# Another written order for the attention and feed-forward stage of a four-stage kernel

## The chip, the cores and the metric

The kernel runs on one core of one Trainium2 chip. A core has five engines that play their own instruction streams side by side: TensorE (PE in the profile; its weight loads are listed apart as PEld), VectorE (DVE), ScalarE (ACT), GpSimd (POOL), and SyncE (SP), which here only issues DMAs. The metric is the device time of one execution in microseconds (us), the median over the runs of one kernel.

## The reference

A sequence of 2048 tokens with 128 channels passes four blocks, each added to its own input. The first is an oscillating recurrence, the second a gated choice among 8 experts, the third a causal attention over 256 tokens. The fourth, which takes two thirds of the time and which the change touches, has six layers of local attention and a feed-forward network:

```python
def attn_layer(x, Wqkv, qs, ksc, Wo):                 # 16 heads of 64
    q, k, v = jnp.split(x @ Wqkv, 3, -1)              # then split into heads
    q, k = l2norm(q) * qs, l2norm(k) * ksc
    q = q * cos * scale + rotate_half(q) * sin * scale
    k = k * cos * inv + rotate_half(k) * sin * inv
    out = local_attention(q, k, v)                    # windows of 32, each sees itself and the one before
    return out @ Wo
...
def ffn_layer(x, g, bln, W1, b1, W2, b2):
    hg = layernorm(x, g, bln) @ W1 + b1
    a, gate = jnp.split(hg, 2, -1)
    return a * jax.nn.gelu(gate, approximate=False) @ W2 + b2
...
for i in range(DEPTH):                                # 6
    x = attn_layer(shift_tokens(x), ...) + x
    x = ffn_layer(shift_tokens(x), ...) + x
```

`shift_tokens` delays half of the channels by one token. All arithmetic of this block is float32.

## The kernel before

Stages 1 to 3 run first and are the same in both kernels. `stage4` keeps the activations transposed (channels on the partitions) in two buffers `s4[0]` (input of a layer) and `s4[1]` (between attention and feed-forward). The tokens are cut into 16 tiles of 128 (`NT`), so that six layers make 96 tiles, and four tiles make a group (`G`), the unit of the feed-forward part.

For each tile there are small step functions (lines 1044 to 1274). Each emits a handful of instructions on one engine:

- `ps` (PE, four matmuls): q and k from `wqkv`; the first digit in a step's name is 0 for q and 1 for k, the second the half. `sq`, `ss` (ScalarE, VectorE): squares and their sums per head; `rn` (POOL): the norms' inverse, a power; `ra`, `rb` (VectorE) and `rs` (POOL): the rotation; `kn` (POOL): k times its norm. `tab` (POOL) makes the rotation's table.
- `pt` (PE, 8 transposes each for q and k), `qT`, `kT` (ScalarE): their copies out of PSUM; `ca` (POOL): the window carried to the next tile.
- `pv` (PE): v; `vt` (ScalarE): its copy; `vw` (SP): v through DRAM into the layout of the windows, by six DMAs.
- `sc` (PE, 128 small matmuls): the scores; `sm`, `mx` (VectorE): mask and maximum; `nb` (POOL); `ex` (ScalarE): 16 exponentials, one for each head; `su`, `nr` (VectorE): sum and division.
- `ptp` (PE, 8 transposes), `pT` (ScalarE): the weights transposed; `po` (PE, 128 small matmuls in four steps `po0` to `po3`): the weighing of v; `oT` (ScalarE): its copy.
- `px` (PE, 64 matmuls for two tiles, so in every other iteration; four steps): the output projection; `s` (VectorE): the residual sum.

For each group (lines 1276 to 1380): `xt` (PE), `xs` (VectorE), `fr` (POOL), `prb` (PE), `xcn` (VectorE): layer norm; `ph` (PE, two matmuls for each of three chunks 0 to 2), `ge` (ScalarE), `act` (the function `gated`, VectorE): the gated hidden layer; `py` (PE, one step for each chunk): the second product; `s2` (VectorE): the sum; `st` (`store`, last layer only: four transposes on PE called `pst`, a copy and a DMA). `bias` runs once a layer.

What sets the order of the work is the list `steps` in `stage4`: pairs of a step and its lag. The loop at its end plays the whole list for each iteration i from 0 to 111; a step with lag d works on tile t = i - d, and a step of a group only where t is a multiple of four. So each iteration is a slice through a pipeline that is 16 tiles deep. Which group steps an iteration holds depends on i mod 4, and `px` plays where t is odd. The helper `InOrder` (line 66) keeps each engine's instructions exactly in the written order, so there is no scheduler that moves them, and the profile shows line 66 for all of them; the tile names tell them apart.

The engines' streams are joined by semaphores and by buffers that come round. All results of PE in stage 4 go through one pool of four PSUM buffers of two banks each, which the tag "big" (line 1037) hands out in the order of the calls: `ps`, `pv`, `pt`, `sc`, `ptp`, `po`, `px`, `xt`, `prb`, `ph`, `py`, `pst` share it. A buffer comes free when its last reader (a copy, mask or sum) is done. Work tiles of ScalarE and VectorE come from a pool of eight (line 1040).

Of the kernel before, what the change touches and what calls it, by code (L numbers as in the profile page):

```python
# [93 lines left out]
class Kernel:  # L94
# [893 lines left out]
    def stage4(self, x3T, out):  # L988
        nc, tc, a = self.nc, self.tc, self.a
        with ExitStack() as ctx:  # L990
# [42 lines left out]
            st = [{} for _ in range(DEPTH * NT + 1)]  # L1033
# [348 lines left out]
            def of(f, *n):  # L1382
                return lambda t: f(t, *n)

            tiles = dict(
                tab=tab, rn=rn, kn=kn, vt=vt, vw=vw, pt0=of(pt, 0), qT=qT, pt1=of(pt, 1), kT=kT, ca=ca,
                sm=sm, mx=mx, nb=nb, ex=ex, su=su, nr=nr, ptp=ptp, pT=pT, oT=oT, s=s,
# [10 lines left out]
            for n in range(3):  # L1398
# [5 lines left out]


            steps = [
                ("ps00", 0), ("pT", 4), ("ps01", 0), ("ph21", 14), ("mx", 3), ("py0", 15), ("xcn", 11), ("rn", 2),
                ("py1", 15), ("nb", 3), ("py2", 15), ("sq0", 0), ("ra1", 1), ("po0", 4), ("po1", 4), ("ge2", 14),
                ("ex", 3), ("rb1", 1), ("rb0", 0), ("po2", 4), ("kn", 2), ("s2", 15), ("tab", -1), ("px0", 5),
                ("px1", 5), ("st", 15), ("px2", 5), ("ra0", 0), ("ph00", 13), ("xt", 9), ("act2", 14), ("xs", 9),  # L1410
                ("ss1", 1), ("px3", 5), ("po3", 4), ("s", 5), ("pt1", 2), ("kT", 2), ("vw", 3), ("ph10", 11),
                ("ph01", 13), ("pt0", 1), ("ph11", 11), ("ca", 3), ("ss0", 1), ("oT", 4), ("pv0", 2), ("qT", 1),
                ("pv1", 2), ("su", 3), ("sc0", 2), ("rs1", 1), ("sc1", 2), ("nr", 3), ("vt", 2), ("sc2", 2),
                ("sc3", 2), ("ge1", 11), ("ge0", 13), ("sm", 2), ("ps10", 0), ("act0", 13), ("ps11", 0),
                ("prb", 10), ("fr", 9), ("act1", 11), ("ph20", 13), ("ptp", 3), ("sq1", 0), ("rs0", 0),
            ]
            last = DEPTH * NT
            self.wo4 = {}
# [121 lines left out]
```

## Time and profile before

| | |
|---|---|
| median of three runs | 2450.68 us (2450.47 to 2456.15) |
| the profiled execution's own time | 2441.8 us |
| its span, from first to last instruction | 2439.8 us |
| TensorE's mean granted clock | 0.969 |
| busy: PE, DVE, ACT, POOL | 91%, 78%, 70%, 64% |
| matmuls on PE | 39448 |
| of stage 4: `ps`, `po`, `pt`, `px` | 768, 12288, 1536, 3072 matmuls |
| DMA | 193.83 MB, mean 79 GB/s |

The profile is of one execution, taken by the hardware profiler. It gives each engine's busy time, the waits with what ended them (the releaser), and a chain of work that ended last, followed back from the last instruction. "issue" means an engine waited for nothing that the profile shows. Three kinds of answers of the trace are used below: sums over a stretch of time, lists of the waits in it, and a timeline, in which neighbouring instructions of one kind are folded into a row with start, duration, engine, operation, result and operands, their partitions and shapes, how many there were, and in brackets the idle time before the first.

### The profile page before, as it was taken

Reading aid. Unit: us, or ns where it says so; the run is one execution under the profiler, and the core shown is the slowest. Engines: PE = TensorE matmul, PEld = TensorE weight load, DVE = VectorE, ACT = ScalarE, POOL = GpSimd, SP = SyncE. Lnnn points to the kernel's source line nnn. Section 1 sums busy time; section 2 is a strip of 40 time slices with the busy share of each in tenths; the row PEclk is TensorE's granted clock in tenths of the full one; section 3 lists DMA queues with packets and bytes.
Section 4 is the critical chain, followed back from the end, with each engine's and each line's share of the span. In section 5 each row is a group of like instructions: output and inputs, shape, how many; then the busy total and the mean of one; then the engine's idle time right before and its main releaser. Section 6 shows DMA issues by size and latency. Waiting matters only on the chain.

```text
span 2439.8 us, 88508 instructions
## 1 busy us (share of the span) xinstructions
PE 2229.9 (91%) x39448; PEld 1380.0 (57%) x39448; DVE 1902.5 (78%) x2743; ACT 1707.6 (70%) x3209; POOL 1573.5 (64%) x1205
## 2 busy tenths in 40 slices
PE   5678889999997799999999999999999999999997
PEld 3663333333334466666666666666666666666664
DVE  7667777776652788888888888888888787888875
ACT  3323455666664678888788888888888787888873
POOL 4244210001122999888888888888888788888870
PEclk8788999999998899999999999999999999999999
DMA  2000000000001544354344444453435443343331
GB/s 82 1 1 1 1 1 2 2 2 2 2 2 44 131 115 115 106 144 111 106 106 141 114 110 120 123 132 104 113 106 136 104 120 98 104 115 107 105 101 50
DMA packets 101021, 193.83 MB, mean 79 GB/s; under 512 B 11480, under 2 KB 32608, under 8 KB 100640
## 3 DMA queue, kind: packets, MB, share of 16 engines
q1 hardware_dynamic: 100060, 187.71, 28.1%
q8 instruction: 310, 5.08, 0.9%
q14 instruction: 71, 0.58, 0.1%
q10 hardware_dynamic: 580, 0.46, 0.1%
HBM read 124.17 MB, written 63.96 MB: 77 GB/s over the span
## 4 chain that ended last, share of the span: by engine, by line
PE 57%; ACT 2%; issue 1%; DVE 1%; POOL 1%; ACTq 0%
PE ps L66 13%; PE po L66 8%; PE px L66 7%; PE pv L66 6%; PE pt L66 6%; PE sc L66 5%; PE ph L66 5%; PE ptp L66 3%; PE py L66 3%; ACT sm L66 1%; PE prb L66 1%; ACT kT L66 1%; PE xt L66 0%; DVE s L66 0%; DVE yT L66 0%
## 5 line engine op out<-in xcount | busy, mean ns | idle before, releaser
L66 POOL TENSOR_TENSOR rn<-ss,mhalf 128x32 f32<-128x32 f32 x96 | 523.9, 5457 | 8.0
L66 ACT ACTIVATE sm<-sm,mx,rn 128x64 f32<-128x64 f32 x1536 | 519.1, 428 | 2.3 <-POOL mx L66 1.8
L66 POOL TENSOR_TENSOR rot_a<-rot_a,rot_b 128x1024 f32<-128x1024 f32 x192 | 452.8, 2371 | 14.5 <-DVE rot_a L66 13.4
L66 DVE TENSOR_REDUCE mx<-sc 128x1 f32<-128x512 f32 (+3 forms) x640 | 355.1, 604 | 120.9 <-PE sc L66 114.0
L66 ACT ACTIVATE ex<-sc 128x512 f32<-128x512 f32 (+3 forms) x640 | 302.9, 536 | 198.8 <-PE sc L66 197.5
L66 PE MATMUL sc<-kT,qT 64*32 64x64 f32 (+3 forms) x14208 | 375.0, 243 | 28.8 <-issue 21.3
L66 PE MATMUL ps<-wqkv,s 128*128 128x512 f32 x768 | 376.4, 613 | 6.3 <-DVE vec L66 2.4
L66 ACT ACTIVATE sq<-ps 128x1024 f32<-128x1024 f32 x192 | 196.6, 1024 | 218.5 <-issue 113.0
L66 PE MATMUL sc<-qT,kT 32*128 32x512 bf16 (+3 forms) x1920 | 248.4, 348 | 23.7 <-DVE mx L66 16.2
L66 DVE TENSOR_TENSOR rot_b<-ps,tab 128x1024 f32<-128x1024 f32 x192 | 229.8, 1216 | 24.6 <-ACT sq L66 22.9
L66 DVE TENSOR_TENSOR rot_a<-ps,tab 128x1024 f32<-128x1024 f32 x192 | 233.5, 1217 | 17.1 <-ACT sq L66 16.5
L66 PEld LDWEIGHTS po<-pT,vw 64*64 64x64 f32 x12288 | 195.6, 135 | 86.6 <-ACT pT L66 41.1
L66 DVE TENSOR_REDUCE ss<-sq 128x16 f32<-128x1024 f32 x192 | 228.4, 1211 | 1.4
L66 PE MATMUL po<-pT,vw 64*64 64x32 f32 x12288 | 214.6, 220 | 3.7 <-ACT pT L66 2.6
L66 PE MATMUL pt<-ident,rot_a 128*128 128x128 f32 x1536 | 199.6, 279 | 15.3 <-POOL rot_a L66 15.3
L66 POOL TENSOR_SCALAR_AFFINE_SELECT ex<-ex 128x512 f32<-128x512 f32 x64 | 40.6, 635 | 267.6 <-ACT ex L66 267.4
L66 PE MATMUL pv<-wqkv,s 128*128 128x512 f32 x384 | 184.0, 602 | 21.1 <-ACT kT L66 20.8
L66 PEld LDWEIGHTS pt<-ident,rot_a 128*128 128x128 f32 x1536 | 172.4, 142 | 45.4 <-issue 18.5
L66 PEld LDWEIGHTS ps<-wqkv,s 128*128 128x128 f32 x768 | 132.2, 192 | 112.9 <-issue 100.1
L66 PE MATMUL px<-oT,wo 64*128 64x128 f32 x3072 | 187.7, 277 | 1.9 <-issue 1.9
L66 PEld LDWEIGHTS sc<-kT,qT 64*32 64x32 f32 x12288 | 128.4, 105 | 101.1 <-issue 89.3
L66 PE MATMUL av<-ex,va 128*32 128x256 f32 (+1 forms) x2432 | 178.5, 372 | 5.0 <-POOL ex L66 5.0
(225 smaller groups left out, 3679.1 us busy)
## 6 DMA issues: line engine op xcount, KB each, us to landing
vw<-vd SPq DMA_DIRECT2D x384, 256.0 KB
vd<-vt SPq DMA_DIRECT2D x96, 512.0 KB
vd<-vt SPq DMA_DIRECT2D x90, 128.0 KB
wqkv<-in_L_ffn_Wqkv SPq DMA_DIRECT2D x18, 512.0 KB
wo<-in_L_ffn_Wo SPq DMA_DIRECT2D x24, 256.0 KB
w<-in_L_ffn_W SPq DMA_DIRECT2D x6, 341.0 KB
x<-in_L_attn_hidden_states SPq DMA_DIRECT2D x4, 256.0 KB
out<-ot SPq DMA_DIRECT2D x4, 256.0 KB
```

What stands on the lines that cost most here:

```text
L66: return self._tc.keep_in_program_order(call(*args, **kw))
```

## The change

Only the list `steps` changes: the order of its entries and some of the lags. Every step is still played once for each tile or group, so both kernels issue the same instructions on the same data, except where a step of one iteration is now played in a neighbouring one.

- `px` stands ahead of `po`, and `po0` to `po3` follow one another; before, `px` stood between `po2` and `po3`. Where i mod 4 is 1, `ph21` stands in the middle of `po`.
- `ph20` stands at the start of an iteration instead of the end, `ph21` has lag 13 instead of 14, `ph00` and `ph01` stand behind `sc` instead of around `xt` and `pt`. `py0` has lag 14 instead of 15. `prb` stands at the start.
- `mx` and `nb` have lag 2 instead of 3, `rn` 1 instead of 2, `pT` 3 instead of 4, each at the end of the iteration instead of near its start; `ss0` has lag 0 instead of 1, `rs0` 1 instead of 0, `xcn` 10 instead of 11, `ge2` and `act2` 13 instead of 14.
- Other entries (`s`, `s2`, `st`, `xs`, `fr`, `ca`, `tab`, `kn`, `qT`, `su`) stand elsewhere in the list with the same lag; the store stands behind `vw` instead of ahead of it.

```diff
--- before.py
+++ after.py
@@ -1404,15 +1404,15 @@
 
 
             steps = [
-                ("ps00", 0), ("pT", 4), ("ps01", 0), ("ph21", 14), ("mx", 3), ("py0", 15), ("xcn", 11), ("rn", 2),
-                ("py1", 15), ("nb", 3), ("py2", 15), ("sq0", 0), ("ra1", 1), ("po0", 4), ("po1", 4), ("ge2", 14),
-                ("ex", 3), ("rb1", 1), ("rb0", 0), ("po2", 4), ("kn", 2), ("s2", 15), ("tab", -1), ("px0", 5),
-                ("px1", 5), ("st", 15), ("px2", 5), ("ra0", 0), ("ph00", 13), ("xt", 9), ("act2", 14), ("xs", 9),
-                ("ss1", 1), ("px3", 5), ("po3", 4), ("s", 5), ("pt1", 2), ("kT", 2), ("vw", 3), ("ph10", 11),
-                ("ph01", 13), ("pt0", 1), ("ph11", 11), ("ca", 3), ("ss0", 1), ("oT", 4), ("pv0", 2), ("qT", 1),
-                ("pv1", 2), ("su", 3), ("sc0", 2), ("rs1", 1), ("sc1", 2), ("nr", 3), ("vt", 2), ("sc2", 2),
-                ("sc3", 2), ("ge1", 11), ("ge0", 13), ("sm", 2), ("ps10", 0), ("act0", 13), ("ps11", 0),
-                ("prb", 10), ("fr", 9), ("act1", 11), ("ph20", 13), ("ptp", 3), ("sq1", 0), ("rs0", 0),
+                ("ps00", 0), ("ps01", 0), ("prb", 10), ("ra1", 1), ("kn", 2), ("ph20", 13), ("rb1", 1), ("rs0", 1),
+                ("tab", -1), ("sq0", 0), ("ca", 3), ("px0", 5), ("py1", 15), ("ex", 3), ("px1", 5), ("py2", 15),
+                ("ra0", 0), ("rs1", 1), ("rb0", 0), ("xt", 9), ("px2", 5), ("px3", 5), ("po0", 4), ("po1", 4),
+                ("ph21", 13), ("po2", 4), ("po3", 4), ("pt1", 2), ("xs", 9), ("xcn", 10), ("fr", 9), ("vw", 3),
+                ("s", 5), ("s2", 15), ("st", 15), ("py0", 14), ("ph10", 11), ("kT", 2), ("ss1", 1), ("pt0", 1),
+                ("oT", 4), ("ph11", 11), ("pv0", 2), ("pv1", 2), ("ss0", 0), ("sc0", 2), ("sc1", 2), ("sc2", 2),
+                ("su", 3), ("qT", 1), ("sc3", 2), ("nr", 3), ("vt", 2), ("ge2", 13), ("sm", 2), ("ph00", 13),
+                ("ge1", 11), ("mx", 2), ("rn", 1), ("ph01", 13), ("ps10", 0), ("ge0", 13), ("ps11", 0),
+                ("act2", 13), ("act0", 13), ("nb", 2), ("act1", 11), ("ptp", 3), ("sq1", 0), ("pT", 3),
             ]
             last = DEPTH * NT
             self.wo4 = {}
```

## The prediction

> **What bounds the kernel now.** I read the page first, then the busy time by stretch, the waits and the timeline of TensorE over stage 4's steady state. The page:
>
> ```profile
> span 2439.8 us, 88508 instructions
> ...
> PE 2229.9 (91%) x39448; PEld 1380.0 (57%) x39448; DVE 1902.5 (78%) x2743; ACT 1707.6 (70%) x3209; POOL 1573.5 (64%) x1205
> ...
> ## 3 DMA queue, kind: packets, MB, share of 16 engines
> ...
> q8 instruction: 310, 5.08, 0.9%
> ...
> PE 57%; ACT 2%; issue 1%; DVE 1%; POOL 1%; ACTq 0%
> ```
>
> By stretch, from 1250 to 2250 us (busy time of PE, PEld, DVE, ACT, POOL), and that stretch's waits (total, times, longest):
>
> ```profile
> 1250.00:2250.00 1000.00, 966.66 (x19936) 664.82 (x19935) 846.95 (x983) 827.23 (x1485) 864.79 (x526) 1.00 0.42 114
> ```
>
> ```profile
> PE sc L66 <- issue: 14.6, 13, 3.9
> PE pv L66 <- ACT kT L66: 13.7, 15, 0.9
> ```
>
> TensorE is 97% busy and the chain runs on it. Its idle time has two parts of equal size: pv (the value projection) waits for ScalarE's copy kT, once per group of four tiles (15 groups here), and sc (the scores) stops with "issue", 13 times. So the order of PE's work, what it waits for, and where it runs out of instructions set the time; the other engines' idle time costs nothing. I name an iteration of the step loop by i mod 4: class 0 to 3. The timeline of class 1, of class 2 and of class 3 (start, duration; durations overlap a little, so I take start to start):
>
> ```profile
> 1566.03 1.88 PE L66 MATMUL ps<-wqkv,s 128*128 128x512 f32 x4
> ...
> 1573.27 1.04 PE L66 MATMUL pt<-ident,rot_a 128*128 128x128 f32 x8
> 1575.22 1.98 PE L66 MATMUL pv<-wqkv,s 128*128 128x512 f32 x4 [0.91 <-ACT kT L66]
> ```
>
> ```profile
> 1584.77 1.60 PE L66 MATMUL po<-pT,vw 64*64 64x32 f32 x96
> 1586.30 3.84 PE L66 MATMUL px<-oT,wo 64*128 64x128 f32 x64
> 1590.07 0.67 PE L66 MATMUL po<-pT,vw 64*64 64x32 f32 x32
> 1590.67 1.97 PE L66 MATMUL pt<-ident,rot_a 128*128 128x128 f32 x16
> 1592.47 1.88 PE L66 MATMUL pv<-wqkv,s 128*128 128x512 f32 x4
> 1594.29 1.45 PE L66 MATMUL sc<-kT,qT 64*32 64x64 f32 x125
> 1596.84 0.30 PE L66 MATMUL sc<-kT,qT 64*32 64x64 f32 x3 [1.10 <-issue]
> ```
>
> ```profile
> 1600.64 1.88 PE L66 MATMUL ps<-wqkv,s 128*128 128x512 f32 x4
> 1602.36 2.74 PE L66 MATMUL py<-act,w 128*128 128x512 f32 x6
> 1605.03 2.07 PE L66 MATMUL po<-pT,vw 64*64 64x32 f32 x128
> 1607.03 1.09 PE L66 MATMUL pt<-ident,rot_a 128*128 128x128 f32 x8
> ...
> 1610.55 1.88 PE L66 MATMUL pv<-wqkv,s 128*128 128x512 f32 x4
> ```
>
> To see: in class 2 po is cut by px (1.53 + 3.77 + 0.60); in class 3 po is whole (2.00); in class 1 PE is done with pt at 1573.27 + 8 x 0.109 = 1574.14 and starts pv at 1575.22; and sc lost 1.10 us three matmuls before its end.
>
> **What the skill says.** "TensorEngine Tiling (Array Packing)", Key Properties: a change of tiling mode drains TensorE. The trace agrees: po in one piece takes 2.00, in two 1.53 + 0.60 = 2.13, so a cut costs 0.13 us. "Runtime: NRT & Kernel Launch", Instruction fetch mechanics: instructions arrive by DMA in blocks of 16 KiB, 256 instructions. The trace agrees in size (5.08 MB / 310 packets = 16 KB; 2 x 39448 / 310 = 254), but not that the fetch is mostly hidden: sc's "issue" stops are such fetches by my count along the program, as they stand where a block's edge falls inside 256 instructions played in 1.4 us. "ScalarE: Activation LUTs", What ACT_TABLE_LOAD costs, gives 1283 ns; the trace has the same mean, and both orders need four per group, so nothing changes.
>
> **The change, part by part.** By position in the written order, classes 0 to 3 hold, on PE between the first ps pair and pt, before: po96 px po32; po96 ph xt po32; ph po96 px po32; py py py po. After: px po; ph xt po64 ph po64; prb px po; py py po.
>
> 1. *px ahead of an uncut po* (classes 0 and 2). 5.90 becomes 3.77 + 2.00 = 5.77: -0.13. 3072 px matmuls of 64 are 48 iterations: **-6.2 us**. px's operand oT was copied an iteration before; po's pT gets 3.8 us more room.
>
> 2. *Hidden steps moved between classes.* ph20/ph21 go from classes 1/2 to class 1 (+0.86 there, -0.86 in class 2), py0 from class 3 to class 2 (+0.86, -0.86), prb only within class 2. The work sums to nothing; what matters is which class then waits.
>
> 3. *Class 3's new wait.* There kT is done when ScalarE has squared (1.02, from 1.92 after ps starts), taken 16 exponentials (5.40 in this iteration) and copied kT: 9.14 us after ps, overlaps deducted. The four PSUM buffers go round so that pv takes pt1's, which kT frees. Before, PE comes to pv at 1610.55 - 1600.64 = 9.91: covered by 0.77. Without py0's 0.86 it comes at 9.05 and waits until 9.19 (in class 1 pv started at 1575.22 - 1566.03 = 9.19): 0.14, and 0.10 more to refill as after class 1's wait: +0.24, 24 groups: **+5.7 us**. Queued behind pv: sc, ps1, ptp. Class 1's own wait stays (PE ready at 8.11 against 8.12).
>
> Per group: -0.13 (class 0), +0.86 (1), -0.13 (2), -0.86 + 0.24 (3) = -0.02, from 64.50 us, the sum of the shortest periods of the four classes. 24 groups: **-0.6 us**. So the steady cycle is even.
>
> 4. *Steps moved on other engines.* On POOL rn, nb, rs0: 14.2 us of work per tile, 15.9 in class 1, in periods of 15.2 to 17.0, so they fit; nb still comes before ex with 2.8 us to spare. mx and pT are written at the end of an iteration instead of the next one's start, the same moment. On DVE xs, s, s2, st (1.75, 0.85, 1.5) change places: s2 before pt0 leaves 0.45, xs before pt0 0.4, rb1 before po 0.33; on ScalarE qT before ps1 in class 0 leaves 0.18, vt before ps1 in class 2 0.25, vt before ph in class 1 0.24. On SP's queue the last layer's store moves behind vw's DMAs, six per tile, which wait only for the vt of an iteration before and are read by po an iteration later, as before. All covered by my timetable, worked from the trace's durations. If a cover of 0.2 is missed by as much, that is 24 x 0.2 = 5 us for one step: 0 to +10, taken **+2**.
>
> 5. *Instruction blocks.* I counted where PE's block edges fall in the two programs. Over stage 4, sc begins 9 times before and 13 after at the places where it always stopped (the edge falls near its end), 15 and 11 where it stopped half the time, 6 and 8 where it rarely did. Before, about 17.5 expected stops cost 25 us with their refills, 1.45 each; after, 13 + 5.5 + 1.5 = 20: +3.6. And po, now 256 instructions in 2.0 us straight after px, has two edges within 3.2 us a dozen times more than before; stops at po and px cost 0.2 to 0.8 in the trace: 0 to +8, taken +3.5. **+7 us**, ends -4 and +18. That is the least known part.
>
> 6. *Ends of the stage.* In the drain (2344 to 2440 us) px now covers a wait of po for pT (1.15 and its restart) and py0 and po are no longer behind a store's transposes (-1.1), but the last py0 waits for its act alone (+0.9): **-1.5**, ends -5 and +1. In the first iterations POOL sets the pace (14.1 us each): 0, plus or minus 1.
>
> Sum: -6.2 + 5.7 - 0.1 (rounding) + 2 + 7 - 1.5 = **+6.9 us** on the profiled execution's 2441.8 (span 2439.8 and 2.0 around it), so 2448.7 there. The runs' median, 2450.68, lies 8.9 above that execution; I add the difference to the median: 2457.6, rounded to **2458**. 0.3% is 7.4 us, about what a measurement of this kernel tells from no change, so the forecast lies right at that bound.
>
> **Rivals.**
> - *Even.* The blocks cost no more than before (0 for part 5) and the waits of part 4 hold: -0.6 - 1.5 = 2448.6; 2444 to 2457 with the small terms. For it: of some 250 edges in stage 4 of the trace, 33 cost anything. Against: four more edges where sc always stopped.
> - *Faster, the other sign: class 3 doesn't wait.* If kT ends 0.14 us earlier there, or pv gets a buffer other than pt1's, +5.7 falls away, and with fewer edges stopping (-2 to -4) 2450.7 - 6.2 - 1.5 - 3 = 2440. It decides at 9.05 us after ps: kT before that, no wait. For it: the margin is only 0.14. Against: class 1's 15 waits for the same kT are alike (13.7 us in all, 0.9 the longest).
> - *Much slower: the small covers fail.* qT or vt, 0.2 late in two or three classes, 0.2 plus 0.1 refill each, or po stopping at most edges: 24 x 0.6 + 7 = +21, 2472. For it: four covers under 0.35. Against: none of these waits is in the trace of before.
> - *No saving from part 1:* if px's entry from a 128-row matmul costs as much as the cut, +6: it adds to the forecast (2464).
>
> **Chances.** Forecast (2453 to 2465, with the last rival) 0.50; even 0.17; faster 0.23; much slower 0.10. Of the forecast's half three quarters lie above 2458.0 (its upper part, the last rival, is included), so slower 0.37 + 0.10 = 0.47; same 0.13 + 0.15 = 0.28; faster 0.23 + 0.02 = 0.25. The range: 2441 leaves out a tenth at the fast end, 2473 a tenth at the slow one.
>
> **What would show it.** px and po in 5.77 start to start; pv in class 3 with an idle of about 0.1 from ACT kT, so twice as many such waits, near 30 in 1000 us; sc's "issue" stops at 15 or more instead of 13; new "issue" stops at po; group periods near 64.5 without stops. A total of PE waits on ACT qT or vt above 3 us would speak for the much slower rival; no wait at class 3's pv and fewer stops would make me wrong on the fast side.

## The result, and the profile after

The changed kernel takes 2464.28 us in the median of 17 runs (2454.33 to 2481.56) against 2451.42 of before in the same runs. The ratio is 1.0058, with a 95% interval of 1.0042 to 1.0073: 14 us slower, with ends of 10 and 18 (the medians are 12.9 us apart). The forecast was 2458 (7 us slower) within 2441 to 2473; direction and range held, the size was half of what came.

The page of the changed kernel: span, TensorE's busy line and, from its costliest groups, the scores and the weighing (busy, mean ns | idle just before them, and what ended most of it).

```profile
span 2462.6 us, 88435 instructions
...
PE 2231.1 (91%) x39448; PEld 1367.4 (56%) x39448; DVE 1938.9 (79%) x2743; ACT 1709.3 (69%) x3209; POOL 1570.9 (64%) x1205
...
L66 PE MATMUL sc<-kT,qT 64*32 64x64 f32 (+3 forms) x14208 | 377.9, 243 | 34.2 <-issue 25.2
...
L66 PE MATMUL po<-pT,vw 64*64 64x32 f32 x12288 | 206.9, 220 | 10.5 <-issue 10.4
```

The same two groups of the kernel before:

```profile
L66 PE MATMUL sc<-kT,qT 64*32 64x64 f32 (+3 forms) x14208 | 375.0, 243 | 28.8 <-issue 21.3
...
L66 PE MATMUL po<-pT,vw 64*64 64x32 f32 x12288 | 214.6, 220 | 3.7 <-ACT pT L66 2.6
```

po is busy 7.7 us less (no cuts), but now stops with "issue" for 10.4 us, which it hardly did before; sc stops for 4 us more. VectorE is busy 36 us more with the same 2743 instructions. Both have to be explained. The waits after, from 1250 to 2250 us (total, times, longest):

```profile
PEld pv L66 <- ACT kT L66: 24.1, 26, 1.2
PE sc L66 <- issue: 14.0, 14, 1.7
PEld ps L66 <- DVE sm L66: 14.0, 15, 1.1
PE pv L66 <- ACT kT L66: 11.6, 14, 1.0
PE po L66 <- issue: 7.8, 9, 1.9
PE pt L66 <- issue: 4.0, 4, 1.3
```

Before, the first of these lines was:

```profile
PEld pv L66 <- ACT kT L66: 17.3, 15, 1.2
```

pv's weight load now waits for kT 26 times instead of 15: class 3 has its wait. New are po's stops and a wait of ps for VectorE's sm, once per group. An iteration of class 0 in the timeline after:

```profile
1905.51 3.84 PE L66 MATMUL px<-oT,wo 64*128 64x128 f32 x64
1909.28 2.05 PE L66 MATMUL po<-pT,vw 64*64 64x32 f32 x123
1912.65 0.31 PE L66 MATMUL po<-pT,vw 64*64 64x32 f32 x5 [1.32 <-issue]
1912.89 1.97 PE L66 MATMUL pt<-ident,rot_a 128*128 128x128 f32 x16
1914.69 1.88 PE L66 MATMUL pv<-wqkv,s 128*128 128x512 f32 x4
1916.51 1.20 PE L66 MATMUL sc<-kT,qT 64*32 64x64 f32 x101
1919.05 0.44 PE L66 MATMUL sc<-kT,qT 64*32 64x64 f32 x27 [1.34 <-issue]
```

po stops five matmuls before its end and sc, one block of 256 instructions later, stops again. Class 1 after, on TensorE:

```profile
2268.03 1.98 PE L66 MATMUL pv<-wqkv,s 128*128 128x512 f32 x4 [0.96 <-ACT kT L66]
2269.94 1.48 PE L66 MATMUL sc<-kT,qT 64*32 64x64 f32 x128
2271.36 1.98 PE L66 MATMUL ph<-xc,w 128*128 128x512 f32 x4
2273.61 1.98 PE L66 MATMUL ps<-wqkv,s 128*128 128x512 f32 x4 [0.27 <-DVE sm L66]
```

and on VectorE and GpSimd in the same iteration:

```profile
2265.84 1.59 DVE L66 TENSOR_SCALAR fmv<-fmv 128x4 f32<-128x4 f32 x1
```

```profile
2265.02 2.38 POOL L66 TENSOR_TENSOR rot_a<-rot_a,rot_b 128x1024 f32<-128x1024 f32 x1
```

The addition of epsilon in `xs`, four numbers per partition, took 1.59 us and ended at 2267.43, when GpSimd's sum `rs1` ended (2267.40). Before, the same two steps stood so:

```profile
1573.02 0.17 DVE L66 TENSOR_SCALAR fmv<-fmv 128x4 f32<-128x4 f32 x1
```

```profile
1570.57 2.36 POOL L66 TENSOR_TENSOR rot_a<-rot_a,rot_b 128x1024 f32<-128x1024 f32 x1
```

There `rs1` had ended at 1572.93, before the addition began. "SBUF — State Buffer" in the Trainium skill, section "SBUF: two separate sides", says that VectorE and GpSimd share a pair of ports as an exclusive lock, held for a whole instruction, for some forms of VectorE's instructions. This trace agrees: over stage 4 the addition took 0.19 us on average before and 1.42 after, and the 22 of the 24 that took over 1.4 us after ended 26 to 32 ns behind the end of a GpSimd instruction.

Where the 22.8 us between the two profiled spans lie, by the starts of the iterations: up to iteration 12, +5.2; iterations 12 to 92, +16.9; 92 to 95, +3.0; from 95 to the end, -2.4. Of the first 5.2, 2.0 lie in stages 1 to 3, whose code is the same, and 3.2 in iterations 0 to 12. The shortest periods of the classes are 15.30, 17.3, 17.04 and 15.21. In the middle of the undisturbed ones class 1 is at 17.4. The forecast's terms, added to the shortest periods before (15.44, 16.06, 17.17, 15.83), gave 15.31, 16.92, 17.04 and 15.21.

TensorE's granted clock is no cause of this distance: it is 0.93 in stages 1 to 3 and 1.00 in iterations 12 to 92 of both profiled executions. But it makes executions of one kernel differ: of the 17 of the changed kernel the slowest, 2481.56 us, had a mean clock of 0.960, and one of 2457.97 us 0.972. In the 14 profiled executions of this document stages 1 to 3 alone, the same code everywhere, take from 786.7 us (clock 0.93) to 794.8 (0.91). Where profiled executions are compared below, iterations 12 to 92 say more than the whole span.

I sum PE's idle times at the edges of the instruction blocks in stage 4 (every 256th instruction, always at place 193 of the trace's order): 27.7 us in 33 stops before, 44.5 us in 46 stops after. I call this sum "the stops" below. Two versions of the kernel before, further down, leave its order on TensorE as it is and have 33.0 and 32.9 us, so a difference of some 5 us between two profiled executions says nothing; the 17 us here are more than that. Where an edge falls matters: of the edges within the last 16 of sc's 128 matmuls every one stopped (9 of 9 before, 13 of 13 after), of those in the first 64 none (of 49 and of 47). Within the last 32 matmuls of a whole po lie 6 edges before, of which 3 stopped, and 21 after, of which 8 stopped.

### The profile page after: what moved, and what is told of

Same layout as the page of the kernel before. It is cut to its first block, busy times and chain, and to the rows that moved or that the text cites. A ratio compares the mean times of both kernels' runs of the same rounds, so it can differ in the third digit from the quotient of the medians.

```text
span 2462.6 us, 88435 instructions
## 1 busy us (share of the span) xinstructions
PE 2231.1 (91%) x39448; PEld 1367.4 (56%) x39448; DVE 1938.9 (79%) x2743; ACT 1709.3 (69%) x3209; POOL 1570.9 (64%) x1205
## 3 DMA queue, kind: packets, MB, share of 16 engines
q1 hardware_dynamic: 100060, 187.71, 27.7%
## 4 chain that ended last, share of the span: by engine, by line
PE 68%; DVE 18%; ACT 7%; issue 3%; POOL 3%; DMA 0%; DVEq 0%; ACTq 0%; POOLq 0%
PE ps L66 13%; PE sc L66 13%; PE px L66 7%; PE po L66 6%; PE pv L66 5%; PE pt L66 5%; PE av L66 5%; DVE mx L66 4%; PE ptp L66 3%; PE py L66 3%; PE ph L66 2%; ACT sm L66 2%; DVE ss L66 2%; DVE fmv L66 2%; DVE rot_a L66 2%
## 5 line engine op out<-in xcount | busy, mean ns | idle before, releaser
L66 PE MATMUL pt<-ident,rot_a 128*128 128x128 f32 x1536 | 203.1, 281 | 19.8 <-POOL rot_a L66 13.2
L66 PE MATMUL po<-pT,vw 64*64 64x32 f32 x12288 | 206.9, 220 | 10.5 <-issue 10.4
L66 PEld LDWEIGHTS px<-oT,wo 64*128 64x128 f32 x3072 | 175.2, 188 | 22.3 <-issue 22.0
```

What stands on the lines that cost most here:

```text
L66: return self._tc.keep_in_program_order(call(*args, **kw))
```

## The experiments

The theories were L (VectorE stands still while GpSimd holds the lock), F (the stops at instruction blocks, with kT's wait: the forecast's terms), and later T (the stops come from fetches that queue behind vw's transfers) against D (they come from the order of PE's instructions alone).

### The lock taken away

```diff
-                dve.tensor_scalar_add(mv[:, :, 1], mv[:, :, 1], EPS)        # in xs
+                gps.tensor_scalar_add(mv[:, :, 1], mv[:, :, 1], EPS)        # at the head of fr
```

> The changed kernel with one edit: the add of epsilon in xs (VectorE, a tensor_scalar on 128x4) is done on GpSimd at the head of fr. Theory L (the lock): VectorE's tensor_scalar in class 1 stands still (1.42 us on average instead of 0.19) while GpSimd plays rs1, and with it all of VectorE's queue, so that ps1 waits for sm; class 1's period falls from 17.4 to 16.9 and the run is 24 x 0.5 = 12 us shorter, about 2452. Theory F (instruction blocks and kT's wait, the forecast's own terms): nothing but places on VectorE changes, 2462 to 2467. In both the class 3 period stays at 15.21.

Ratio 1.0060 (1.0043 to 1.0077): nothing gained. Yet class 1's shortest period is 16.92, the forecast's value to the hundredth, and ps's weight loads wait 4.8 us for sm instead of 14.0. Iterations 12 to 92 are 1.9 us shorter. The stops are 49.5 us, 5 more, most of the difference at po (16.4 instead of 10.5); that is no more than two profiled executions of one order differ, so where the 12 us went isn't shown.

The second edit, to the scalings:

```diff
-                    dve.tensor_scalar_mul(qks[:, 0:2], qks[:, 0:2], QK_SCALE)        # in tab, and the two below it
+                    gps.tensor_scalar_mul(qks[:, 0:2], qks[:, 0:2], QK_SCALE)
```

> The edit of the run before, and the three scalings of qks at a layer's start (tensor_scalar on 128x64 and 128x128) moved from VectorE to GpSimd as well. Theory L: these three stand still too (0.73 us on average instead of 0.19) at the five layer edges inside the stage, where class 3 takes 16.33 instead of 15.21: another 5 x 1.1 = 5.6 us, about 2446 in all. Theory F: 2462 to 2467. If GpSimd's own extra work of some 1 us at the edge comes onto the path instead, about 2452.

Ratio 1.0034 (1.0016 to 1.0052), so 6 us less than the changed kernel's 1.0058 (1.0042 to 1.0073); the intervals overlap, so the size is uncertain. Iterations 12 to 92 are 7.7 us shorter. The period of class 3 at the layer edges (15, 31, 63, 79; the fifth, 47, had a stop in it) is 15.21 instead of 16.33 to 16.37. Stops: 43.8.

> Control: both edits on the kernel before. Theory L: there the add of epsilon takes 0.19 us and the scalings 0.19 us, so nothing stands still and nothing is gained: within 3 us of 2451. Theory F: the same. A gain of 5 us or more would mean that the edit helps by itself and the first two runs say nothing about the change.

Ratio 0.9990 (0.9973 to 1.0007), as expected of the control, with 33.0 us of stops. Theory L is shown for the mechanism and its size in the periods; for the time, only about 6 of the 18 us that the periods show came back.

### px ahead of an uncut po, alone

In the kernel before:

```diff
-                ..., ("po0", 4), ("po1", 4), ..., ("po2", 4), ...
-                ("ss1", 1), ("px3", 5), ("po3", 4), ...
+                ("ss1", 1), ("px3", 5), ("po0", 4), ("po1", 4), ("po2", 4), ("po3", 4), ...
```

> The kernel before with one part of the change alone: po0 to po2 moved down beside po3, so that px stands ahead of an uncut po. The prediction's part 1: 5.90 becomes 5.77 in classes 0 and 2, 48 times 0.13, so -6 us (2445), if the instruction blocks stop PE as often as before. If contiguous po behind px brings more stops (part 5), up to 10 us slower than that, with class minima of 15.31 and 17.04 all the same. If the cut costs nothing, the minima stay at 15.44 and 17.17.

Ratio 1.0069 (1.0048 to 1.0090): 17 us slower, where the saved cuts alone would give 6 faster. The shortest periods of classes 0 and 2 are 15.30 and 17.03, so the 0.13 are there; the stops doubled to 55.5 us, 58 of them. Within the last 32 matmuls of a whole po now lie 26 edges instead of 6, and 20 of them stopped, 16.0 us:

```profile
L66 PE MATMUL po<-pT,vw 64*64 64x32 f32 x12288 | 208.6, 221 | 19.8 <-issue 19.6
```

The stops aren't all of it. The part from iteration 95 on takes 108.9 us instead of 103.1: 4.9 of the stops lie there instead of 0.1, and the last layer's store, which here stands ahead of all of po, has its transposes wait 12.6 us for yT instead of 9.5. And the granted clock was lower, 0.9635 on average in this kernel's 13 runs against 0.9670 in the 66 of before; in the profiled execution of this kernel it was 0.991 in iterations 12 to 92 instead of 0.997, by my estimate up to 8 us (0.9% of 1355.3 against 0.3% of 1334.8). Whether the order lowers the clock, or chance did, stays open.

### The cut put back into the changed kernel

```diff
-                ("px0", 5), ..., ("px3", 5), ("po0", 4), ("po1", 4), ("ph21", 13), ("po2", 4), ("po3", 4),
+                ("po0", 4), ("po1", 4), ("ph21", 13), ("po2", 4), ("px0", 5), ..., ("px3", 5), ("po3", 4),
```

> The changed kernel with px put back between po2 and po3. Theory F (instruction blocks): contiguous po behind px is what makes PE run out of instructions; with the cut back, the 'issue' stops of PE in stage 4 fall from 44 us to about 34, as before, and the cut costs 48 x 0.13 = 6 us: 2460, 4 below the changed kernel's 2464. Rival S (the cut itself is the only price, part 1 without part 5): 6 us slower than the changed kernel, 2470, with the same stops.

Ratio 1.0125 (1.0092 to 1.0158): 16 us slower than the changed kernel's ratio, against both expectations. The stops didn't fall: po's went from 10.5 to 6.6, sc's from 25.3 to 31.6, px's from 0 to 4.3:

```profile
L66 PE MATMUL sc<-kT,qT 64*32 64x64 f32 (+3 forms) x14208 | 379.1, 243 | 41.0 <-issue 31.6
```

Only 9 edges lie in the last 32 matmuls of a whole po now, and none stopped; but sc keeps 13 edges in its last 16, as in the changed kernel (before: 9), and 11 of them stopped. So "uncut po" is not by itself the cause of the stops. The cut's own price, S, is there: of the 15.5 us between the two profiled spans 6.0 lie in iterations 12 to 92. Another 8.3 lie ahead of iteration 12, 4.1 of them in stages 1 to 3, where the clock was 0.92 instead of 0.93. The mean clock of this kernel's 6 runs is that of the changed kernel's 17 (0.967), so what else makes the runs 16 us slower isn't shown. With the lock taken away as well:

> The changed kernel with both VectorE scalings and the add of epsilon on GpSimd and px between po2 and po3: the three costs found so far undone together. By the sum of the shortest periods (15.44 + 16.92 + 17.17 + 15.21 = 64.74 against 64.50 before) 6 us slower than before, with stops as before (about 34): 2457. If something else is left in the changed order, more than 2460.

Ratio 1.0087 (1.0056 to 1.0117), 21 us above before where 6 was the sum: stops 46.5, sc again 31.3, with the same 13 edges in its last 16 matmuls.

### Class 3's wait

In the changed kernel:

```diff
-                ("py0", 14), ...
+                ("py0", 15), ("py1", 15), ...
```

> The changed kernel with py0 back at lag 15, so that class 3 has py0, py1 and py2 ahead of po again. Part 3 of the prediction: class 3's wait for kT (0.14 and 0.10) goes; class 3 15.21 becomes 15.83, class 2 17.04 becomes 16.17: 0.24 x 24 = 6 us less, 2458. If part of what is saved is eaten by more stops, between 2458 and 2464. If class 3 had no wait of its own, 2464.

Ratio 1.0042 (1.0025 to 1.0059): 4 us less than the changed kernel, which the runs alone don't tell from nothing (its interval begins at 1.0042). The periods do: class 3 15.83, class 2 16.18, as worked out, and pv's wait for kT is back at one per group:

```profile
PEld pv L66 <- ACT kT L66: 16.4, 15, 1.2
```

### Class 1's wait in the kernel before

ex is played in two parts, with kT between them where i mod 4 is 1:

```diff
+                ("exa", 3), ..., ("pt1", 2), ("ka", 2), ("exb", 3), ("kT", 2),        # ka: kT if t % 4 == 3; exa: heads 0 to 11
```

> The kernel before with one edit on ScalarE: in class 1 the copy kT is played after 12 of ex's 16 exponentials instead of behind all of them. If class 1's wait of pv for kT is the price that the profile shows (0.91 idle, 1.0 to 1.1 start to start), class 1 falls from 16.06 to about 15.0 and the run by 24 x 1.05 = 25 us to 2426. If what is saved goes into instruction stops instead, as the first four runs suggest for other savings, a half: 2438. If pv's start then waits on something else (oT's or qT's buffer), 2445 or more.

Ratio 0.9984 (0.9963 to 1.0006). The wait for kT is gone, but sc then waits for the buffer that oT frees and ps1 for vt's, so class 1 is 15.48 and not 15.0: 24 x 0.58 = 14 us, of which at most 9 came, 4 by the middle; the stops are 32.9. Moving oT too:

> The kernel before; in class 1 the copies oT and kT are played on ScalarE after 8 of ex's 16 exponentials. Class 1 was 15.48 with kT alone early, where sc waited 0.26 for oT's buffer: now about 15.2, so 24 x 0.85 = 20 us less than before if all of it showed, and 4 to 10 us less if stops eat as much as in the run with kT alone (1 to 4 of 14 us). This is the version that could beat both kernels.

Ratio 1.0012 (0.9997 to 1.0027): nothing. Class 1 is 16.11, since ps now waits for vt, whose copy comes later:

```profile
PE ps L66 <- ACT vt L66: 9.6, 14, 0.7
```

No version here beats both kernels clearly.

### Without the transfers of vw

What holds a block up? The profile has the packets that bring the blocks (16 KB each, on a DMA queue of their own). In the changed kernel 16.7 of the 44.5 us of stops followed a microsecond in which the DMA engines were over 80% busy before the block's own packet started; in 44 of the 46 stops PE went on 1.1 to 1.8 us after that packet's end, wherever it started. Three kernels leave vw's transfers out after two tiles (33.6 MB of DMA in all instead of 193.8):

```diff
             def vw(t):
+                if t > 1:
+                    st[t]["vw"] = st[t % 2]["vw"]
+                    return
```

> The kernel before without the transfers of vw (v through DRAM) after the first two tiles: po reads the v of tiles 0 and 1 again, so this part of the computation is left out; no engine's work but the DMAs changes. Theory T (instruction blocks arrive late because they queue behind these transfers): the 'issue' stops of PE in stage 4, 28 us in the profile of before, of which 7.5 us followed a microsecond in which the DMA engines were over 80% busy, fall to about 18, and the run by 8 to 10. Theory D (the stops depend on PE's instruction density alone): stops and time as before.

> The changed kernel with the same part left out. Theory T: its stops fall from 44.5 us (16.7 of them behind busy DMA engines) to about 27, and the run by some 17 us, so that the distance to the kernel before without vw shrinks from 14 us to about 7. Theory D: the distance stays at 14.

> The kernel before with px ahead of an uncut po, and without the vw transfers: the run that lost 17 us against before with its transfers. Theory T: its stops fall from 55 us (27.5 behind busy DMA engines) to about 28, and the distance to the kernel before without vw is within 5 us, the 6 us of the saved cuts against some more stops. Theory D: still 17 us slower than before without vw.

| kernel | ratio with vw | ratio without | stops with | stops without |
|---|---|---|---|---|
| before | 1 | 0.9881 | 27.7 us, 33 | 13.8 us, 13 |
| changed | 1.0058 | 1.0006 | 44.5 us, 46 | 23.5 us, 23 |
| px first | 1.0069 | 0.9963 | 55.5 us, 58 | 25.4 us, 23 |

Without the transfers the stops fall by half in all three, and po's all but vanish. The scores and the weighing in the changed kernel without vw:

```profile
L66 PE MATMUL sc<-kT,qT 64*32 64x64 f32 (+3 forms) x14208 | 377.6, 243 | 27.7 <-issue 20.0
...
L66 PE MATMUL po<-pT,vw 64*64 64x32 f32 x12288 | 203.6, 220 | 0.0
```

the scores in the kernel before without vw:

```profile
L66 PE MATMUL sc<-kT,qT 64*32 64x64 f32 (+3 forms) x14208 | 374.1, 243 | 19.3 <-issue 11.8
```

and the weighing with px first, without vw (with it, 19.8 above):

```profile
L66 PE MATMUL po<-pT,vw 64*64 64x32 f32 x12288 | 201.3, 221 | 0.5 <-issue 0.5
```

But the edit does more than leave out transfers: TensorE's waits for them go too. Its semaphore instructions in stage 4 fall from 444 to 417 (before), 490 to 422 (changed) and 444 to 374 (px first), so the edges of its blocks fall elsewhere. The stops have to be compared at like places: edges within the last 32 matmuls of sc or of a whole po, how many of them stopped, and for how long in all:

| kernel | sc with vw | sc without | po with vw | po without |
|---|---|---|---|---|
| before | 16 of 24, 19.7 us | 9 of 21, 11.7 us | 3 of 6, 1.0 us | 0 of 5 |
| changed | 20 of 23, 22.4 us | 16 of 24, 20.0 us | 8 of 21, 9.1 us | 0 of 22 |
| px first | 17 of 24, 20.1 us | 14 of 20, 19.6 us | 20 of 26, 16.0 us | 2 of 25, 0.5 us |

For po theory T is shown: at like places 28 of 47 edges stopped with the transfers in the last two kernels, 2 of 47 without. For sc it is not: an edge there costs 0.88 us on average with them and 0.79 without, and most of what sc saves in the first two kernels comes with fewer edges in its last 16 matmuls (5 instead of 9, 7 instead of 13), which speaks for theory D.

Theory T is also wrong on the difference between the kernels: the distance from before to the changed kernel grows to 27.4 us (2448.16 against 2420.76) instead of shrinking to 7. That number can be put together: the lock in class 1, 24 x 0.5 = 12; the lock at five layer edges, 5 x 1.1 = 5.6; stops, 23.5 - 13.8 = 9.7; the rest of the cycle, -0.6. Sum 26.7. (The profiled pair is 29.7 apart, of which 4.2 lie in stages 1 to 3; stage 4's share is 25.5.) So without transfers the terms add, and with them 14 us is left of the same terms. For px first the distance is 20 us; 11 of it lie in the end of the stage (112.3 us from iteration 95 on against 101.3). There the granted clock was 0.85 in this execution and 0.93 in the other, by my estimate up to 10 us (15% of 112.3 against 7% of 101.3), so that the store ahead of po need not be the cause.

## Why the prediction was right, and where it was off

1. *px ahead of an uncut po, -6.2.* Right in the periods: 15.30 and 17.04 against 15.31 and 17.04. Alone, it cost 17 us all the same, with 28 us more of stops.
2. *Steps moved between classes sum to nothing.* Right: class 2 and class 3 came out to the hundredth.
3. *Class 3's new wait, +5.7.* Right: 15.21, and 26 waits of weight loads instead of 15. When py0 was put back the two periods together fell by 0.24, as forecast; the runs show 4 us, about their own uncertainty.
4. *Steps moved on other engines, all covered, +2.* This failed. The timetable took 0.17 us for the addition of epsilon, from a trace in which GpSimd's rs1 had just ended; in the new order it falls inside rs1 and takes 1.42 on average. VectorE's chain ss, su, nr, sm behind it is late, and ps1, behind ph00 and ph01, waits for the buffer that sm frees: 17.4 for 16.92, 12 us; the scaling of qks at the layer edges is caught in the same way, 5.6 us. Neither was in the forecast.
5. *Instruction blocks, +7, ends -4 and +18.* The mechanism was right and the size too small: the stops rose by 16.8 us in the profiled pair. sc's part was well sized (21.3 to 25.3, +4.0 against +3.6), and its edges were counted right: 9 and then 13 at the places where they always stop. The stops at other steps rose from 6.4 to 19.2 us, against +3.5: 13 at po cost 0.8 each, the upper end of what I had read from the trace of before, and pt stopped too.
6. *Ends of the stage, -1.5.* -2.4 from iteration 95 on; but the first 12 iterations, taken at 0, cost 3.2 more, with 2.5 of the stops in them.

The sum was +6.9; it came to +14. The two terms that were too small, 4 and 5, would give 12 + 5.6 + 16.8 in place of 2 + 7, which is 25 more than was forecast, so they overlap: by 9 in the profiled pair, which is 22.8 apart, and by 18 against the medians, where the profiled execution of before (2441.8) was a quick one. How they overlap isn't shown; a stop in class 1 ahead of pv, for instance, could be hidden in kT's wait. So the right direction rests on more cost than I saw and less of it arriving: that the time came within the range is in part luck. Why a cut of po loses in the new order and its absence in the old one is answered in part: the old order without the cut puts 20 more edges at the end of a whole po, and in the new one the cut costs its own 6 us while sc's 13 late edges stay. The times at which the packets start, which the transfers bear on, were not controlled here.

The rivals: "even" and "faster" are refuted, class 3 waits. "Much slower" had the kind right (a cover that fails in one class of iterations) and the place wrong: ps1 waits for sm, not for qT or vt. "No saving from part 1" is refuted by the periods. Of the signs named beforehand, the saving at px and po, the new stops at po and nearly twice as many waits of pv for kT came; sc's stops in the 1000 us were 14, not 15 or more.

## What to carry to other kernels

An instruction's duration from a trace holds for its neighbours in that trace: before VectorE and GpSimd steps are moved against each other, look for small VectorE instructions that end when a GpSimd instruction ends. Where TensorE plays hundreds of small matmuls in a row, add up its stops at the 256-instruction edges, count the edges that fall near the end of such a row, and compare both between orders; a saving of tenths of a microsecond per iteration can be eaten by them. A sum of shortest periods is a bound, not a forecast, when such stops make up several tens of microseconds. And an edit that takes out waits moves every later edge, so stops are to be compared at like places.

## What was not expected of the hardware

An addition of four numbers per partition on VectorE took up to 1.60 us while GpSimd ran. At the end of po TensorE's stops for instructions went away with the transfers of vw (28 of 47 edges, then 2 of 47). The kernel before lost 27 us with these transfers, 1.2%, though the DMA engines were only 42% busy; the stops fell by 13.9 us, and where the rest came from isn't shown.
